# A cross-attention kernel: the value products are issued after the pair of value projections of their quarter, next to the score wave that follows

## The chip, the cores and the metric

The kernel runs on one core of one Trainium2 chip. The time is the device time of one execution in microseconds (us). Before the change it was 1936.94 us, the median of three runs (1934.74 to 1937.29). The profile was taken of a further execution, which took 1937.88 us, of which 1936.1 us lie between its first and its last instruction (the span). The engines are named as in the profile: PE multiplies matrices, PEld loads PE's weights, DVE and POOL work on vectors, ACT does activations and copies and issues some DMAs, SP issues the other DMAs.

## The reference

Three layers are computed for 16 batches of 64 query rows of width 1024: cross attention to a context of 1024 rows per batch, self-attention with rotary positions, and a quantized feed-forward layer. The change lies in the first one.

```python
def _L0_xattn_ref(query, key, value, Wq, Wk, Wv, Wo):   # key = value = the context
    q = (query @ Wq).reshape(b, sq, 32, 32).transpose(0, 2, 1, 3)
    k = (key @ Wk).reshape(b, sk, 8, 32).transpose(0, 2, 1, 3)
    v = (value @ Wv).reshape(b, sk, 8, 32).transpose(0, 2, 1, 3)
    k = jnp.repeat(k, 4, axis=1)
    v = jnp.repeat(v, 4, axis=1)
    scores = jnp.einsum('bhqd,bhkd->bhqk', q, k) * 32 ** (-0.5)
    probs = jax.nn.softmax(scores, axis=-1)
    out = jnp.einsum('bhqk,bhkd->bhqd', probs, v)
    return out.transpose(0, 2, 1, 3).reshape(b, sq, 1024) @ Wo

x = x + _L0_xattn_ref(_layernorm(x), ctx, ctx, Wq, Wk, Wv, Wo)
x = x + attn(_layernorm(x))
x = x + ffn(_layernorm(x))
```

## The kernel before

The program is recorded in the order in which the code issues it (`manual_schedule`, line 905): each engine executes its own instructions in that order, and semaphores are set wherever one needs what another makes. So the order of the Python calls is the order of the work on each engine.

**Units and slots.** Cross attention is cut into 32 units, one for each batch and each half of the heads (`class Unit`, line 416). The loop at line 939 runs 32 slots. In slot n the unit n is finished while the scores of unit n+1 (`following`) are made; slot n therefore holds work of two units. The profile's span from 187 us to 1340 us is this loop up to its last slot. A slot has four quarters, i = 0 to 3 (line 963). In each quarter these come in turn on PE:

- a *wave* of scores for the following unit (`by_key`, line 421; matmuls of line 430): eight products of 32 rows by 128 columns of weights with 256 columns of queries. Four of them use four row groups of the array side by side. The scores lie in two PSUM tiles of one buffer each, from which ACT copies them (line 442) while DVE keeps a running maximum over keys (lines 446 and 449). The next wave can only be written when both have read this one.
- two *fillers* (`fill`, line 900), taken from a list. In slots 0 to 29 the list holds the projections of the next batch's context: in quarters 0 and 1 the two halves of one 128x512 key projection each (line 225), in quarters 2 and 3 two *value steps* each, `v_0` to `v_3` (`values` within `project`, line 308; eight 128x128 products with 256 columns, line 311, then a copy by ACT, line 318). They share two PSUM banks (`ps_m`), taken in turn. In slots 30 and 31 the fillers are halves of the output projection of the first tiles (`project_out`, line 523) and a layer norm.
- between the two fillers, in quarters 2 and 3, the *value products* of unit n (`Unit.values`, line 484; matmuls of line 491): 16 products of a 128x32 weight with 256 columns of probabilities, four side by side in four column groups. Quarter 2 has the waves 0 and 1, quarter 3 the waves 2 and 3. In quarter 0 of the next slot, behind its two fillers, `finish` (line 499) adds the sums of probabilities (line 501) and divides (line 508).

One matmul of the code is recorded twice (the operands are 32-bit), so 8 products of a value step are 16 records, a wave has 16 and the value products of a quarter 32.

**The softmax and its detour through memory.** `exponentials` (line 472) subtracts the maxima on DVE (line 475), takes the exponential on ACT (line 476) and adds on POOL (lines 479 and 482). The maxima must be the same for all partitions. At the end of quarter 3, `reduce` (line 451) brings them together on DVE, its last instruction being line 461. Then ACT's queue writes 4 KB of them to device memory (`spread`, line 467) and reads them back into all partitions (`everywhere`, line 470). Below this write and this read are called the *bounce*. ACT's copies of the next wave stand behind both in ACT's order, so they wait until the write has landed.

**Loads.** The context comes in halves of 2 MB (`load_context`, line 290; the DMA is issued on SP's queue, line 207) into two buffers that are used in turn. At the start of an even slot the half for the next odd slot is issued; it overwrites the half that the four value steps of the odd slot just ended have read, and SP waits for the last of those matmuls. SP also carries the weight pieces of the feed-forward layer that are treated along the way (`load_piece`, line 365: 688 KB at line 369; from slot 8 on they are also written back, line 386).

The p buffers (`p_ring`, line 190: seven places, four per unit) are written by ACT's copies of line 442; the copies of wave 3 take the place of wave 0 of the unit that is being finished, which the value products of quarter 2 read.

Of the kernel before, what the change touches and what calls it, by code (L numbers as in the profile page):

```python
# [49 lines left out]
def kernel(  # L50
# [151 lines left out]
    def load_x(dst, t):  # L202
        nc.sync.dma_start(dst, x[bass.ts(t, P), :])

    def load(src):
        st = stream.next([KC, 512])
        nc.sync.dma_start(st, src)
        return st
# [81 lines left out]
    def load_context(b, h):  # L290
        ctx_halves[b, h] = load(ctxT[b, h])

    def project(b):


        kT = kv_ring.next([2, NK])
        v = kv_ring.next([8, KVD])
        key_steps, value_steps = [], []

        def keys(h, g):  # L300
            return matmul_steps(
                lambda: m_tile(f"k_{b}_{h}_{g}"),
                lambda k: wkvs[:, k, bass.ts(g, P)],
                lambda k: ctx_halves[b, h][:, k, :],
                lambda ps: nc.scalar.copy(kT[:, g, bass.ts(h, 512)], ps),
            )

        def values(h, kt):
            ps = m_tile(f"v_{b}_{h}_{kt}")
            for k in range(KC):  # L310
                nc.tensor.matmul(  # L311
                    ps[:, :KVD],
                    lhsT=ctx_halves[b, h][:, k, bass.ts(kt, P)],
                    rhs=wkvs[:, k, KVD:],
                    start=(k == 0),
                    stop=(k == KC - 1),
                )
            nc.scalar.copy(v[:, h * 4 + kt, :], ps[:, :KVD])  # L318

        for h in range(2):  # L320
            key_steps.append(keys(h, 0) + keys(h, 1))
            value_steps.append([lambda h=h, kt=kt: values(h, kt) for kt in range(4)])
        return kT, v, key_steps, value_steps
# [48 lines left out]
    def treat_piece():  # L372
        if not loaded:
            return
        i, m, c, st = loaded.pop(0)
        if i < len(pieces_of_w):
            nc.scalar.activation(st, st, AF.Abs, accum_out=asum[:, m, c : c + 1])
        else:


            nc.scalar.activation(
                st, st, AF.Identity, scale=inverse[:, m : m + 1], bias=magic[:, 0:1]
            )
            q = place(ternary_at, [HALF], F8)
            nc.scalar.activation(q, st, AF.Sign, bias=magic[:, 1:2], saturate=False)
            nc.sync.dma_start(half_of(ternary[m][c // 2], c), q)
        if i + 2 not in (len(pieces_of_w), len(pieces_of_w) + 1):
            load_piece(i + 2)
# [134 lines left out]
    def project_out(t, h):  # L523
        cols = bass.ts(h, 512)
        return matmul_steps(
            lambda: m_tile(f"wo_{t}_{h}"),
            lambda k: outputs[k // 4][:, t, k % 4, :, :],
            lambda k: wos[h][:, k, :],
            lambda ps: nc.vector.tensor_tensor(xs[t][:, cols], ps, xs[t][:, cols], ALU.add),
        )  # L530
# [20 lines left out]
    def norm2(t):  # L551
        n2s[t] = n2_ring.next([DIM])
        for step in layernorm(n2s[t], xs[t], f"n2_{t}"):
            step()
# [345 lines left out]
    def fill(n=1):  # L900
        for _ in range(n):
            if fillers:
                fillers.pop(0)()

    with tc.manual_schedule():
# [14 lines left out]
        unit, last = Unit(0, kT, v), None  # L920
# [18 lines left out]
        for n in range(2 * B):  # L939

            b = n // 2
            if n % 2 == 0:
                fill(len(fillers))
                if b + 1 < B:
                    load_context(b + 1, 1)
                    kT, v, key_steps, value_steps = project(b + 1)
                    tiles.append((kT, v))
                    for h in range(2):
                        fillers += key_steps[h] + value_steps[h]
                else:  # L950
                    for t in range(4):
                        load_x(xs[t], t)
                    nc.sync.dma_start(wkvs2, wkv2)
                    for h in range(2):
                        for t in (4, 5):
                            fillers += project_out(t, h)
                    for t in (0, 1):
                        for h in range(2):
                            fillers += project_out(t, h)
                        fillers += [lambda t=t: norm2(t)]  # L960
            following = Unit(n + 1, *tiles[(n + 1) // 2]) if n + 1 < 2 * B else None

            for i in range(4):
                if following:
                    following.by_key(i)
                    if i == 3:
                        following.reduce()
                if n < 8 or i % 2 == 0 and (n, i) != (8, 0) or i == 3 and n % 2 == 1:
                    treat_piece()
                if n == 8 and i < 2:  # L970
                    (thresholds, thresholds_end)[i]()
                if i == 1 and n % 2 == 1:

                    if b + 2 < B:
                        load_context(b + 2, 0)
                    elif b + 2 == B:
                        wos.append(load(wo[0]))
                fill()
                if i == 1:
                    unit.exponentials(0)  # L980
                if i == 2:
                    unit.exponentials(2)
                    unit.values((0, 1))
                if i == 3:
                    unit.values((2, 3))
                if following and i == 3:
                    following.spread()
                fill()
                if following and i == 3:
                    following.everywhere()  # L990
                if last and i == 0:
                    last.finish()
                if i == 1:
                    unit.exponentials(1)
                if i == 2:
                    unit.exponentials(3)
            if n == 2 * B - 4:
                for t in (4, 5):
                    load_x(xs[t], t)
            if n == 2 * B - 3:  # L1000
                wos.append(load(wo[1]))
            if n == 2 * B - 2:
                for t in (6, 7):
                    load_x(xs[t], t)
            last, unit = unit, following
# [194 lines left out]
```

## Time and profile before

| | us |
|---|---|
| median of three runs | 1936.94 |
| profiled execution | 1937.88 |
| its span | 1936.1 |
| PE busy in the span | 1906.5 (98%) |
| DVE busy | 1162.8 (60%) |
| ACT busy | 893.5 (46%) |
| POOL busy | 835.9 (43%) |
| key projections on PE (line 225, k) | 472.2 |
| value projections (line 311) | 460.5 |
| score waves (line 430) | 146.7 |
| value products (line 491) | 125.5 |
| sum products (line 501) | 20.4 |

The busy times are unions of overlapping instructions: a matmul record of 379 ns does not mean that the next one starts 379 ns later. What one more matmul costs is read from the distance between starts. The granted clock of PE was 0.997 of full speed on the mean. "idle before" counts the idle time of an engine just before a group and names what ended it; an idle time of DVE, ACT or POOL matters only where PE then waits for them.

### The profile page before, as it was taken

The page shows a single profiled execution, that of the slowest core. Times are in us where ns is not written, and L with a number is a line of the kernel's source. Part 1 is how long each engine was busy: PE and PEld are TensorE (multiplying, and loading weights), DVE is VectorE, ACT ScalarE, POOL GpSimd, SP SyncE. Part 2 cuts the span into 40 slices and gives each one's busy share as a digit, 9 for nine tenths or more (in the row PEclk, how much of TensorE's full clock was granted, in tenths as well). Part 3 has the DMA queues.
Part 4 walks back from the last instruction along what each step waited for, and adds up shares of the span by engine and source line. Part 5 has one row for each costly group of instructions (what it writes and reads, how often), then busy time and mean ns, then how long its engine had stood idle before and what let it go on. Part 6 is the DMA issues. An engine that isn't in the chain of part 4 may idle for free.

```text
span 1936.1 us, 27466 instructions
## 1 busy us (share of the span) xinstructions
PE 1906.5 (98%) x11632; PEld 1112.1 (57%) x11632; DVE 1162.8 (60%) x1336; ACT 893.5 (46%) x972; POOL 835.9 (43%) x411
## 2 busy tenths in 40 slices
PE   8999999999999999999999999999899999999999
PEld 5445566566556656656665565564346464666654
DVE  3012777777677767767767676777424245665564
ACT  1243665666566666666656666543101022333221
POOL 1000466456446546645654565466302423444420
PEclk9999999999999999999999999999999999999999
DMA  8224344353343342343343333314011000122201
GB/s 333 73 88 170 103 169 141 126 174 110 118 166 110 120 172 97 123 164 110 128 146 125 113 110 129 119 55 166 8 48 44 0 30 1 31 74 89 85 23 55
DMA packets 47946, 205.52 MB, mean 106 GB/s; under 512 B 7056, under 2 KB 16208, under 8 KB 42832
## 3 DMA queue, kind: packets, MB, share of 16 engines
q1 hardware_dynamic: 40528, 184.77, 27.4%
q10 hardware_dynamic: 7296, 19.01, 2.9%
q8 instruction: 91, 1.49, 0.3%
q14 instruction: 31, 0.25, 0.0%
HBM read 190.98 MB, written 12.78 MB: 105 GB/s over the span
## 4 chain that ended last, share of the span: by engine, by line
PE 83%; DVE 9%; ACT 3%; DMA 3%; issue 1%; POOL 0%; ACTq 0%; DVEq 0%; POOLq 0%
PE k L225 19%; PE v L311 18%; PE q L225 11%; PE t L430 6%; PE wo L225 5%; PE o L491 5%; PE gu L809 4%; PE d L883 4%; DVE arena L475 4%; PE g L809 3%; DMA tops<-arena 2%; DVE arena L449 2%; ACT arena L476 1%; PE v L589 1%; ACT arena L442 1%
## 5 line engine op out<-in xcount | busy, mean ns | idle before, releaser
L482 POOL TENSOR_TENSOR arena<-arena 128x1024 f32<-128x1024 f32 x192 | 574.3, 2991 | 24.9 <-ACT arena L476 9.9
L225 PE MATMUL k<-arena 128*128 128x512 f32 x1056 | 472.2, 600 | 0.0
L311 PE MATMUL v<-arena 128*128 128x256 f32 x1984 | 460.5, 385 | 0.0
L311 PEld LDWEIGHTS v<-arena 128*128 128x128 f32 x1984 | 367.0, 190 | 90.1 <-issue 45.1
L475 DVE TENSOR_TENSOR arena<-arena 128x2048 f32<-128x2048 f32 x128 | 364.0, 2882 | 0.0
L479 POOL TENSOR_TENSOR arena<-arena 128x1024 f32<-128x1024 f32 x32 | 77.6, 2426 | 650.9 <-ACT arena L476 449.7
L449 DVE TENSOR_TENSOR arena<-t,arena 128x512 f32<-128x512 f32 x384 | 262.3, 689 | 151.7 <-ACT arena L442 99.7
L225 PEld LDWEIGHTS k<-arena 128*128 128x128 f32 x1056 | 195.9, 190 | 242.1 <-issue 236.0
L476 ACT ACTIVATE arena<-arena 128x2048 f32<-128x2048 f32 x128 | 244.8, 1912 | 177.2 <-DVE arena L475 177.2
L442 ACT COPY arena<-t 128x1024 f32<-128x1024 f32 x256 | 248.7, 1012 | 167.0 <-DMA tops<-arena 89.6
L225 PE MATMUL q<-arena 128*128 128x512 f32 x512 | 225.4, 596 | 0.6 <-ACT arena L262 0.6
L446 DVE TENSOR_REDUCE arena<-t 128x512 f32<-128x1024 f32 x64 | 78.0, 1224 | 215.3 <-PE t L430 120.2
L225 PEld LDWEIGHTS q<-arena 128*128 128x128 f32 x512 | 95.3, 190 | 115.9 <-issue 113.7
L430 PE MATMUL t<-arena 32*128 32x256 f32 x2048 | 146.7, 400 | 4.1 <-DVE arena L446 4.1
L430 PEld LDWEIGHTS t<-arena 32*128 32x128 f32 x2048 | 92.5, 184 | 68.2 <-issue 47.6
L491 PE MATMUL o<-arena 128*32 128x256 f32 x2048 | 125.5, 384 | 6.1 <-ACT arena L476 6.1
L809 PEld LDWEIGHTS <-arena 128*128 128x128 bf16 x1024 | 97.6, 97 | 55.0 <-issue 5.0
L821 POOL TENSOR_TENSOR arena<-arena 128x344 f32<-128x344 f32 x64 | 70.8, 1108 | 104.8 <-DVE arena L818 95.5
L225 PE MATMUL wo<-arena 128*128 128x512 f32 x256 | 114.9, 604 | 0.0
L318 ACT COPY arena<-v 128x256 f32<-128x256 f32 x124 | 45.8, 369 | 117.9 <-DVE arena L461 90.4
L491 PEld LDWEIGHTS o<-arena 128*32 128x32 f32 x2048 | 59.8, 110 | 63.6 <-issue 17.6
L508 DVE RECIPROCAL arena<-o 128x256 f32<-128x256 f32 x32 | 56.2, 1755 | 64.9 <-PE o L501 64.7
(129 smaller groups left out, 1559.4 us busy)
## 6 DMA issues: line engine op xcount, KB each, us to landing
arena<-in_ctxT SPq DMA_DIRECT2D x31, 2048.0 KB, 9.0
arena<-in_wg SPq DMA_DIRECT2D x32, 688.0 KB, 4.2
arena<-in_wu SPq DMA_DIRECT2D x32, 688.0 KB, 4.2
arena<-in_wd SPq DMA_DIRECT2D x32, 688.0 KB, 4.2
arena<-tops ACTq DMA_DIRECT2D x32, 512.0 KB, 4.0
arena<-ternary SPq DMA_DIRECT2D x32, 344.0 KB, 3.6
ternary<-arena SPq DMA_DIRECT2D x48, 172.0 KB, 1.9
arena<-in_x SPq DMA_DIRECT2D x16, 512.0 KB, 9.9
```

The lines of the kernel that those rows point to most:

```text
L225: nc.tensor.matmul(made[0], lhsT=lhsT(k), rhs=rhs(k), start=(k == 0), stop=(k == KC - 1))
L311: nc.tensor.matmul(ps[:, :KVD], lhsT=ctx_halves[b, h][:, k, bass.ts(kt, P)], rhs=wkvs[:, k, KVD:], start=(k == 0), stop=(k == KC - 1),)
L430: nc.tensor.matmul(ws[jj // 2][:, jj % 2, a, :], lhsT=self.kT[rows, self.g, bass.ts(i * 2 + a, P)], rhs=qa[self.g][rows, bass.ts(self.b, 2 ...
L442: nc.scalar.copy(pt[:, 2 * mine : 2 * mine + 2], ws[mine])
L446: nc.vector.tensor_reduce(m, w.rearrange("p j a c -> p j c a"), AX.X, ALU.max)
L449: nc.vector.tensor_tensor(m, w[:, :, a], m, ALU.max)
L475: nc.vector.tensor_tensor(pt, pt, by.to_broadcast([P, 4, 2, 256]), ALU.subtract)
L476: nc.scalar.activation(pt, pt, AF.Exp)
L479: nc.gpsimd.tensor_tensor(acc, pt[:, :, 0], pt[:, :, 1], ALU.add)
L482: nc.gpsimd.tensor_tensor(acc, acc, pt[:, :, a], ALU.add)
L491: nc.tensor.matmul(self.po[bass.ts(jj, HD), 0:256], lhsT=self.v[:, kt, bass.ts(self.g * 4 + jj, HD)], rhs=self.pts[i][:, jj, a, :], start= ...
L809: nc.tensor.matmul(ps[:, :CW], lhsT=xqT[t][:, k, :], rhs=wbs[n][i][:, k, :], start=(k == 0), stop=(k == KC - 1),)
```

## The change

The value products of quarters 2 and 3 move from their place between the two fillers of the quarter to a place behind the second filler, so that they stand directly before the next wave (or before the next slot's first wave). The two value steps of the quarter then follow one another. Within quarter 2 they also come behind `exponentials(3)`, whose instructions run on DVE, ACT and POOL. The number of instructions on every engine is the same, and the orders of DVE, ACT, POOL and SP are as before; only PE's order differs.

```diff
@@ -980,9 +980,6 @@
                     unit.exponentials(0)
                 if i == 2:
                     unit.exponentials(2)
-                    unit.values((0, 1))
-                if i == 3:
-                    unit.values((2, 3))
                 if following and i == 3:
                     following.spread()
                 fill()
@@ -994,6 +991,9 @@
                     unit.exponentials(1)
                 if i == 2:
                     unit.exponentials(3)
+                    unit.values((0, 1))
+                if i == 3:
+                    unit.values((2, 3))
             if n == 2 * B - 4:
                 for t in (4, 5):
                     load_x(xs[t], t)
```

PE's order in quarter 2 of slots 0 to 29, before and after (`t` a wave, `v` a value step, `o` value products):

```
before: t_2  v_0  o(0,1)  v_1  t_3
after:  t_2  v_0  v_1  o(0,1)  t_3
```

In slot 31, which has no following unit, the order of the last fillers (`wo` half steps) and value products changes in the same way:

```
before: o(0,1)  wo wo  o(2,3)  wo wo ...
after:  wo  o(0,1)  wo wo  o(2,3)  wo ...
```

## The prediction

> **What bounds the kernel now.** First the windows of two neighbouring slots (columns: stretch, its length, busy time of PE, PEld, DVE, ACT, POOL, granted clock, DMA share, GB/s):
>
> ```profile
> 599.41:636.21 36.80, 36.80 (x232) 22.37 (x230) 27.14 (x27) 25.85 (x24) 20.60 (x9) 1.00 0.38 128
> 636.21:673.90 37.69, 37.40 (x236) 22.66 (x232) 27.45 (x27) 22.57 (x22) 20.45 (x9) 1.00 0.37 132
> ```
>
> PE has no gap in the first and 0.29 us in the second; DVE works 27 us of 37. So PE's order is what counts, and I read PE's timeline (start, length, line, records):
>
> ```profile
> 173.00 13.98 PE L311 MATMUL v<-arena 128*128 128x256 f32 x64
> ...
> 614.65 1.15 PE L430 MATMUL t<-arena 32*128 32x256 f32 x16
> 615.73 3.72 PE L311 MATMUL v<-arena 128*128 128x256 f32 x16
> 619.38 1.93 PE L491 MATMUL o<-arena 128*32 128x256 f32 x32
> 621.25 3.72 PE L311 MATMUL v<-arena 128*128 128x256 f32 x16
> 624.90 1.15 PE L430 MATMUL t<-arena 32*128 32x256 f32 x16
> ...
> 643.28 0.64 PE L501 MATMUL o<-arena,ones 128*32 128x256 f32 x8
> 644.20 1.15 PE L430 MATMUL t<-arena 32*128 32x256 f32 x16 [0.29 <-DVE arena L446]
> ```
>
> A lone value step takes 3.65 us to the start of what follows (619.38 - 615.73); four without a break take 13.90 (to the wave at 186.90), 3.48 each. The last line shows the one place where PE waits regularly: wave 1 of an even slot, for DVE's reading of wave 0. The chain of waits says why:
>
> ```profile
> 606.01 0.61 PE o L501 x8
> 606.65 1.77 DVE arena L508
> ...
> 634.88 0.37 DVE arena L461
> 635.27 6.16 DMA tops<-arena
> 641.46 0.33 ACTq L470
> 641.88 1.02 ACT arena L442
> 642.92 1.24 DVE arena L446
> 644.20 1.15 PE t L430 x16
> ```
>
> From the sum products of the odd slot to wave 1 of the even slot runs a path of DVE, the bounce and ACT that is as long as PE's own work. 6.16 us of it is a 4 KB write. The queues show what it meets (SP, then ACT):
>
> ```profile
> 634.21 0.42 SPq L369 DMA_DIRECT2D arena<-in_wg  x1
> 635.24 0.33 SPq L207 DMA_DIRECT2D arena<-in_ctxT  x1
> 680.84 0.39 SPq L207 DMA_DIRECT2D arena<-in_ctxT  x1
> ...
> 673.31 0.33 ACTq L467 DMA_DIRECT2D tops<-arena  x1
> 674.67 0.33 ACTq L470 DMA_DIRECT2D arena<-tops  x1
> ```
>
> At the end of the even slot nothing is loaded and the write is over in 1.36 us (673.31 to 674.67). At the end of the odd slot (635.27) a weight piece and a 2 MB context half were issued 1.06 and 0.03 us before it.
>
> **The change, part by part.** *PE's switches.* By the starts of single records, matmuls of a value step follow one another in 216 ns; the first takes 320 and the last 309 until the next shape starts. Waves and value products enter and leave in the same way. The order t v o v t has four switches, t v v o t three: one exit (309 - 216 = 93 ns) and one entry (320 - 216 = 104 ns) fall away, 0.197 us a quarter. That presumes that o to t, which the trace does not have, costs what it did after v. Nearest rows: line 501, the same 128x32 shape, to a wave takes 309 ns where PE does not wait, and that wave is again 1.08 us long. Bounds: nothing saved, or a further 197 ns if o to t needed no switch; I take the row. Two quarters make 0.394 us a slot: PE's share of a slot falls from 37.33 (644.20 to the next wave 1 at 681.53) to 36.94.
>
> *Odd slots.* Wave 1 of slots 1 to 27 is reached with 2.4 to 5.1 us to spare after DVE's line 446. All of the saving counts: 14 x 0.394 = 5.5 us.
>
> *Even slots.* Here the path competes. Measured from wave 1 to wave 1 it takes, in slots 2, 4, 6, 8: 37.28, 37.10, 37.39, 36.80; 10 to 26: 37.84, 37.68, 37.64, 36.83, 37.58, 37.68, 37.96, 39.54, 37.06; 28 and 30: 36.12, 36.30; slot 29, where an output weight is loaded instead, 37.41. A slot takes the larger of this and PE's need. If the path stays, the gain is the sum of max(37.33, path) - max(36.94, path), 2.1 us, not 16 x 0.394.
>
> *But the path moves.* The context half is released by the last matmul of v_3. That used to end with the quarter; now o(2,3) follows, 1.86 us, and the whole slot is 0.39 shorter, so it is free some 2.3 us before the bounce. In slots 10 to 26 SP itself arrives at line 207 only 0.54 us before the bounce, behind the weight piece; in 2 to 8, 28, 29 and 30 the full 2.3 us count. What an earlier load does to the 4 KB write I read from the DMA packets, engine by engine. Issued 0.03 to 0.05 us ahead, one context packet of 16 KB (611 ns) stands before the write's first packet, behind 6 to 8 packets of the weight piece; issued 0.10 to 0.11 ahead (slots 2 to 8), three do. Lead costs queue. Each of the write's two packets and its completion then lets one more context packet past. How long can the queue get? The 512 KB read-backs at the starts of slots 8, 28 and 30 were issued into long queues: on the mean of the engines 67, 66 and 69 KB in 11 to 13 packets stood before their first one, which came 2.9 us later than in a free queue. Today's write in slots 10 to 26 has 48 to 57 KB in 7 to 8 packets before it and comes 2.4 to 2.8 us late. If a queue is full at some 67 KB, there is room for about 13 KB, 0.5 us at 16 KB in 611 ns. If it is full at a count, there is room for up to four context packets, 2.4 us. Below nothing the shift can go as well, since a load begun earlier also ends earlier: with 2.3 us of lead perhaps to -1 us. I take 0.5 in slots 10 to 26, because the delay, too, is already within half a us of the full queues', and 0.3 in the others. Then the even slots lose 3.6 us instead of gaining 2.1.
>
> [...] Here packets of the two queues alternate singly once both are there.
>
> *Slots 30 and 31.* In slot 30 one switch goes (0.2) and so does the wait of o(2,3) for its exponential (0.29): 0.5 us. In slot 31 PE stands still for an exponential:
>
> ```profile
> 1371.31 1.93 PE L491 MATMUL o<-arena 128*32 128x256 f32 x16 [5.00 <-ACT arena L476]
> ```
>
> A half output step (8 records, 8 x 0.43 = 3.4 us) now comes before this wait instead of after the last one. The exponentials there hang on DVE and POOL, not on PE's order, so the step is free: 3.4 us, bounded by nothing and 5.0.
>
> *Added waits.* v_1 now starts 1.87 us earlier and needs its bank from the key copy (line 305); in slots 10 to 30 this ends 1.08 to 1.5 us before that (0.89 in slot 9). Behind v_1 would wait all of PE, one for one. o(0,1) comes later, which only eases its wait for exponentials; ACT's copies of wave 3, which reuse what o(0,1) reads, need wave 3 anyway, which PE starts after it. DVE, ACT and POOL keep their orders.
>
> **Sum.** 5.5 - 3.6 + 0.5 + 3.4 = 5.8 us off the profiled execution's 1937.9, 1932.1. That execution stood 0.9 above the median: 1931.
>
> **Rivals.** *The bounce is pushed out (slower).* One mechanism: the context half, freed by v_3 before o(2,3), takes the queue in front of the write. At 2.0 us in slots 10 to 26 (0.7 to 0.9 elsewhere) the even slots lose 19.5 us; against 9.4 gained that is +10.1. PE then idles 2.6 to 3.0 us in six of these nine; one idle time of 2.14 us (slot 24) was followed by 3.41 us at half clock in which the key matmuls lost 1.78 us, one of 2.03 us (at 1638.65) was not, so I add half of the six: +5.3. 1952, with 1943 to 1964 for shifts of 1.5 to 2.4 and no or all clocks lost. It decides from a shift of about 1.0 us. For it: lead visibly costs queue, 0.54 us is ten times the present lead, and single engines of the read-backs had up to 17 packets in front. Against: present writes already come nearly as late as the read-backs in full queues. [...]
>
> *The bounce does not move or gets shorter (faster).* 5.5 + 2.1 + 0.5 + 3.4 = 11.5: 1925; for it, that the half's packets cannot start earlier behind the weight piece. A shift of -0.5 would make it 1920.
>
> *A wash.* A shift of 0.7 to 1.3 gives 1933 to 1941.
>
> *The change does not do what it says*, because o to t costs a switch more than the row of line 501 says. Then PE saves nothing, only 3.9 us of slots 30 and 31 are left, and the earlier release still costs: inside the wash or above it.
>
> **How the numbers follow.** Forecast 0.46 (own range 1927 to 1934), pushed-out bounce 0.34, unmoved 0.10, wash 0.10. Time 1931. 0.2%, 3.9 us, is about what a measurement of this kernel can tell from no change. Faster: 0.41 of the forecast and the unmoved 0.10, 0.51; same: 0.05 and 0.10, 0.15; slower 0.34. The range, 1925 to 1955, leaves out half of the unmoved case and the last third of the pushed-out one.
>
> **What would show it.** PE's timeline: v x32 in 7.10 us and a quarter of 10.04. SP's line 207 should be issued 0.5 us before line 467 at odd slots' ends in slots 10 to 26, and no more right after PE's wave. The write's landing there tells the rivals apart: 6.1 us now, 6.6 by forecast, 8.1 by the rival. PE's idle time before line 430, 4.1 us in all now, should be near 14; near 29 and with more half clock the rival holds. At 1371 a wait of 1.5 us. Wrong would be PE waits before line 311 or a quarter still of 10.24.

## The result, and the profile after

Fourteen runs of the changed kernel have a median of 1935.24 us (1928.31 to 1940.67), fourteen of the kernel before 1937.00 (1934.74 to 1941.34). The ratio is 0.9987 with a 95% interval of 0.9975 to 0.9999: some 2.5 us less, between 0.2 and 4.8. That is less than the 0.2% (3.9 us) which the prediction took as the least that can be told from no change; the forecast was 1931, with the range from 1925 to 1955. The profiled execution took 1936.34, its span is 1934.5.

The profile's rows of the waves and the value products before the change (busy time, mean ns of one, idle time before them and what ended it):

```profile
L430 PE MATMUL t<-arena 32*128 32x256 f32 x2048 | 146.7, 400 | 4.1 <-DVE arena L446 4.1
...
L491 PE MATMUL o<-arena 128*32 128x256 f32 x2048 | 125.5, 384 | 6.1 <-ACT arena L476 6.1
```

The summary of the engines and three of the costliest groups after the change:

```profile
PE 1894.6 (98%) x11632; PEld 1117.2 (58%) x11632; DVE 1162.1 (60%) x1336; ACT 891.2 (46%) x972; POOL 835.1 (43%) x411
...
L311 PE MATMUL v<-arena 128*128 128x256 f32 x1984 | 444.4, 382 | 0.0
...
L430 PE MATMUL t<-arena 32*128 32x256 f32 x2048 | 146.6, 400 | 15.7 <-DVE arena L446 15.6
...
L491 PE MATMUL o<-arena 128*32 128x256 f32 x2048 | 124.8, 384 | 5.0 <-ACT arena L476 5.0
```

PE has 11.9 us less to do (1906.5 before): 60 quarters with 0.197 us saved in each make 11.8. But the span fell by 1.6 only, so PE stands still 10.3 us longer, and the line of the waves shows where: 4.1 us of waits before, 15.7 after, 15.6 of them for DVE's line 446. Two windows in the two slots that the prediction started from (the columns as there; neither these windows nor the prediction's have their borders at waves):

```profile
598.50:635.44 36.94, 36.94 (x233) 22.84 (x232) 27.53 (x28) 25.75 (x24) 20.80 (x8) 1.00 0.39 136
635.44:673.90 38.46, 37.20 (x234) 22.89 (x233) 27.59 (x28) 22.69 (x22) 20.45 (x7) 1.00 0.34 122
```

PE is never idle in the first and for 1.26 us in the second. From wave 1 to wave 1, the odd slot (11) fell from 37.33 to 36.94 us, as worked out; the even one (12) grew from 37.69 to 38.26. PE's timeline shows both the shorter quarter and the wait:

```profile
614.09 7.17 PE L311 MATMUL v<-arena 128*128 128x256 f32 x32
621.20 1.93 PE L491 MATMUL o<-arena 128*32 128x256 f32 x32
623.06 1.15 PE L430 MATMUL t<-arena 32*128 32x256 f32 x16
...
643.14 1.15 PE L430 MATMUL t<-arena 32*128 32x256 f32 x16 [1.25 <-DVE arena L446]
```

From the value steps to the wave after the value products (614.09 to 623.06) it is 8.97 us, and the wave before takes 1.07: a quarter of 10.04. And the chain of waits at the end of that odd slot, with SP's queue for the same stretch:

```profile
633.26 0.38 DVE arena L461
...
633.66 6.71 DMA tops<-arena
...
641.86 1.24 DVE arena L446
```

```profile
632.59 0.42 SPq L369 DMA_DIRECT2D arena<-in_wg  x1
633.11 0.39 SPq L207 DMA_DIRECT2D arena<-in_ctxT  x1
```

The context half is issued 0.55 us ahead of the write (633.11 to 633.66; before, 0.03), and the write of 4 KB lands after 6.71 instead of 6.16.

Cut at fixed points of PE's timeline, the two profiled executions differ as follows (wave 1 of unit 2 is in slot 1, wave 1 of unit 31 in slot 30, the first transposition of the second layer is the first record of line 260 behind slot 31):

| stretch, us | before | after | of it at half clock, before and after |
|---|---|---|---|
| start to wave 1 of unit 2 | 232.37 | 231.39 | |
| to wave 1 of unit 31 (the loop) | 1089.33 | 1089.52 | 3.4 and 3.4 |
| to the first transposition (slots 30 and 31) | 84.74 | 82.26 | 6.8 and 3.4 |
| to PE's end (the tail) | 525.87 | 527.59 | 0 and 3.4 |

Of the first line's 0.98 us, 0.39 are slot 1's saving. The rest, 0.59, lies ahead of the loop, where both kernels run the same instructions; this stretch differs by up to 1.7 us among the ten profiles of this document. The loop gains nothing. What the change brings comes from slots 30 and 31, and 1.7 us of it are lost again in a tail that runs the same instructions, to a stretch at half clock.

### The profile page after: what moved, and what is told of

It is laid out like the page before. It is cut to its first block, busy times and chain, and to the rows that moved or that the text cites. A ratio compares the mean times of both kernels' runs of the same rounds, so it can differ in the third digit from the quotient of the medians.

```text
span 1934.5 us, 27466 instructions
## 1 busy us (share of the span) xinstructions
PE 1894.6 (98%) x11632; PEld 1117.2 (58%) x11632; DVE 1162.1 (60%) x1336; ACT 891.2 (46%) x972; POOL 835.1 (43%) x411
## 4 chain that ended last, share of the span: by engine, by line
PE 72%; DVE 16%; ACT 5%; DMA 5%; issue 2%; POOL 0%; ACTq 0%; DVEq 0%; POOLq 0%
PE k L225 16%; PE v L311 13%; PE q L225 11%; DVE arena L475 6%; PE wo L225 5%; PE t L430 5%; DMA tops<-arena 4%; DVE arena L449 4%; PE d L883 4%; PE gu L809 4%; PE o L491 4%; PE g L809 3%; ACT arena L476 2%; ACT arena L442 2%; PE v L589 1%
## 5 line engine op out<-in xcount | busy, mean ns | idle before, releaser
L311 PE MATMUL v<-arena 128*128 128x256 f32 x1984 | 444.4, 382 | 0.0
L311 PEld LDWEIGHTS v<-arena 128*128 128x128 f32 x1984 | 372.0, 190 | 68.5 <-issue 20.4
L430 PE MATMUL t<-arena 32*128 32x256 f32 x2048 | 146.6, 400 | 15.7 <-DVE arena L446 15.6
```

Source lines behind the costliest of these rows:

```text
L311: nc.tensor.matmul(ps[:, :KVD], lhsT=ctx_halves[b, h][:, k, bass.ts(kt, P)], rhs=wkvs[:, k, KVD:], start=(k == 0), stop=(k == KC - 1),)
L430: nc.tensor.matmul(ws[jj // 2][:, jj % 2, a, :], lhsT=self.kT[rows, self.g, bass.ts(i * 2 + a, P)], rhs=qa[self.g][rows, bass.ts(self.b, 2 ...
```

## Experiments

Eight kernels were run, each timed in five rounds beside the kernel before. "Loop" is the second stretch of the table above.

| run | median (lowest to highest) | ratio to before, 95% | loop |
|---|---|---|---|
| after, half later (e1) | 1919.83 (1917.91 to 1921.48) | 0.9908, 0.9894 to 0.9921 | 1074.45 |
| before, half later (e2) | 1931.90 (1931.00 to 1932.61) | 0.9970, 0.9958 to 0.9982 | 1082.89 |
| quarter 2 alone (e3) | 1947.74 (1944.97 to 1951.11) | 1.0057, 1.0043 to 1.0070 | 1097.09 |
| quarter 3 alone (e4) | 1941.66 (1933.87 to 1946.82) | 1.0018, 1.0004 to 1.0031 | 1093.66 |
| half behind the read (e5) | 1920.52 (1919.96 to 1923.67) | 0.9911, 0.9898 to 0.9925 | 1073.75 |
| slot 31 alone (e6) | 1933.94 (1930.64 to 1939.16) | 0.9986, 0.9976 to 0.9995 | 1087.81 |
| slots 0 to 30 alone (e7) | 1936.41 (1931.99 to 1939.38) | 0.9994, 0.9985 to 1.0003 | 1088.14 |
| all loads behind the read (e8) | 1917.93 (1916.28 to 1920.91) | 0.9897, 0.9881 to 0.9914 | 1071.19 |

**The load in front of the write (e1, e2).** The theory: what the change saves on PE in the loop is lost to the context half, which now passes ahead of the write. The rival: the path over DVE and ACT would bound the even slots anyway. Both orders of PE were run with the half issued later:

```diff
                 if b + 1 < B:
-                    load_context(b + 1, 1)
                     kT, v, key_steps, value_steps = project(b + 1)
...
                     (thresholds, thresholds_end)[i]()
+                if i == 1 and n % 2 == 0 and b + 1 < B:
+                    load_context(b + 1, 1)
```

> The changed kernel, but the context half of the even slot is issued in that slot's quarter 1 instead of at its start, some 9 us after the bounce. Theory A (the gain of the switches is eaten by the write of the bounce, which queues behind the context half that v_3 now frees earlier): the write lands in 1.3 to 3 us at the ends of odd slots instead of 6 to 8, wave 1 of even slots never waits, every slot takes 36.94 us, loop from wave 1 of unit 2 to wave 1 of unit 31 29 x 36.94 = 1071 us against 1089.3 before and 1089.5 after; total near 1917. Theory B (the path of DVE and ACT bounds the even slots whatever the queue holds): the even slots stay at 37.5 to 38.5, total within 3 us of 1935.

> The kernel before, with the context half of the even slot issued in quarter 1. Theory A: the 6.8 us that the loop before spends over 29 x 37.33 go, total near 1930, and no more, since PE's order bounds it then. Theory B: same time as before, 1937.

The first took 1919.83, the second 1931.9. In the first the write lands after 1.4 to 2.7 us in slots 2 to 6 (taking the slot that follows it) and after 2.1 to 4.9 in slots 10 to 26, where the weight piece still stands ahead of it, and wave 1 does not wait there. It waits in four slots only (8, 28, 29 and 30, which take 0.66, 1.34, 0.99 and 0.26 us more than 36.94), at whose beginnings nothing holds SP back and a 2 MB load still goes out 2.1 to 2.4 us ahead of the write. In the second no wave waits, and the loop, 1082.89, is 29 x 37.33 = 1082.6 and 0.3 in slot 9: PE's order alone. So the path never bounds by itself; the write behind the load does. With that gone, the change is worth 8.4 us in the loop by the two runs, and 11.7 against the last run below, of 29 x 0.394 = 11.4 counted.

**One quarter at a time (e3, e4).** In the first only the value products of quarter 2 move, in the second only those of quarter 3 (both diffs against the kernel before). The forecast's mechanism needs quarter 3: there o(2,3) comes behind v_3 and v_3 ends earlier.

```diff
                     unit.exponentials(2)
-                    unit.values((0, 1))
                 if i == 3:
                     unit.values((2, 3))
...
                     unit.exponentials(3)
+                    unit.values((0, 1))
```

```diff
                     unit.values((0, 1))
-                if i == 3:
-                    unit.values((2, 3))
                 if following and i == 3:
...
                     unit.exponentials(3)
+                if i == 3:
+                    unit.values((2, 3))
```

> Only the value products of quarter 2 are moved, those of quarter 3 stay between the value steps, so that v_3 still ends the slot and the context half is released as before. Theory A: 0.197 us a slot from PE, the write lands as before (5 to 6.5 us); odd slots -2.8, even slots about -1.2, slot 31 -3.4: total near 1930. Theory B, in which only the number of switches counts: the loop is the same as with quarter 3 alone.

> Only the value products of quarter 3 are moved: the same 0.197 us a slot from PE, but the context half is released before them as in the changed kernel. Theory A: the write lands in 6 to 8 us, wave 1 of even slots waits as in the changed kernel; odd slots -2.8, even slots +5.5 to +6, slot 31 near 0: total near 1940, slower than quarter 2 alone by some 7 us in the loop up to slot 30. Theory B: the loop is the same as with quarter 2 alone.

The second's time came out as expected, 1941.66: half of the saving, all of the loss. The first missed by 18 us: 1947.74, the slowest of all, so that the expected order of the two is reversed. Two things went against it in its profiled run (1944.97). Slots 30 and 31 take 85.55 us, 0.8 more than before, instead of gaining 3.4: PE's wait before wave 1's products in slot 31 falls to 1.56, but a new one of 5.83 stands before wave 2's. And the loop takes 7.8 us more than before instead of 4 less. SP's queue and ACT's for the end of slot 5 of that run:

```profile
410.20 0.33 SPq L207 DMA_DIRECT2D arena<-in_ctxT  x1
```

```profile
410.52 0.33 ACTq L467 DMA_DIRECT2D tops<-arena  x1
418.18 0.33 ACTq L470 DMA_DIRECT2D arena<-tops  x1
```

And the same places of the changed kernel:

```profile
407.62 0.33 SPq L207 DMA_DIRECT2D arena<-in_ctxT  x1
```

```profile
409.99 0.33 ACTq L467 DMA_DIRECT2D tops<-arena  x1
416.59 0.33 ACTq L470 DMA_DIRECT2D arena<-tops  x1
```

With quarter 2 alone the half goes out 0.32 us (410.20 to 410.52) ahead of the write (0.10 before, 2.37 after the change), and the write takes 7.58 us, a microsecond more than after the change. The lead is not fixed by o(2,3) alone: the write hangs on DVE's path, v_3 on PE, and the 0.2 us that PE saves here bring v_3 forward by as much against the write. What the lead does, by the time from the write's issue to its first packet, is this (slots counted by the one that follows):

| lead of the half, us | slots 2 to 8: first packet, landing | lead | slots 10 to 26, behind a weight piece: first packet, landing |
|---|---|---|---|
| none ahead (e8) | 0.82 to 0.83; 1.34 to 3.05 | none ahead (e8, seven slots) | 2.0 to 2.3; 3.3 to 4.4 |
| 0.10 (before) | 2.7 to 2.8; 5.2 to 5.7 | 0.03 to 0.05 (before) | 2.8 to 3.3; 5.3 to 8.0 |
| 0.31 (e3) | 3.7 to 4.4; 6.1 to 7.6 | 0.22 to 0.26 (e3) | 3.3 to 4.0; 5.9 to 7.8 |
| 2.37 (after) | 3.4 to 3.5; 5.9 to 6.7 | 0.55 (after, six slots) | 3.5 to 3.9; 6.2 to 8.2 |

In slots 2 to 8 the delay rises steeply within the first third of a microsecond of lead and is smaller again at 2.4. So the shorter lead was worse there: 4.9 of the 7.8 us that the loop loses with quarter 2 alone are lost in these four slots. Behind a weight piece the two leads (0.22 to 0.26 and 0.55) delay the write about alike, but after the change only in six of the nine slots. Why a longer lead costs less in slots 2 to 8 is open.

**Parts of the change (e6, e7).** Slot 31 alone, and slots 0 to 30 alone:

```diff
                     unit.exponentials(2)
+                if i == 2 and following:
                     unit.values((0, 1))
-                if i == 3:
+                if i == 3 and following:
                     unit.values((2, 3))
...
                     unit.exponentials(3)
+                if i == 2 and not following:
+                    unit.values((0, 1))
+                if i == 3 and not following:
+                    unit.values((2, 3))
```

That is the edit for slot 31; the other has `following` and `not following` exchanged.

> The kernel before, with the value products behind the second filler in slot 31 alone, where no unit follows. Theory A (the half output step fills PE's wait for an exponential, as forecast): PE's wait of 5.0 us before the value products of waves 2 and 3 falls to 1.6, the loop is as before; 3.3 us less, 1933.6, a ratio of 0.9983. Theory B (the wait is given back later in the tail, or by a stretch at half clock after the new waits): the two norms and transposes that follow end at the same time; 1936 to 1938.

> The changed order in slots 0 to 30, the old one in slot 31. Theory A (odd slots gain 5.5 us, even slots lose 4 to 5.6 because the write is late in slots 2 to 8 and 28 to 30 as well): the loop ends 0 to 1.5 us earlier than before, 1935.5 to 1937. The forecast on record (even slots lose 3.6, slot 30 gains 0.5) would make it 1934.5. Theory B (the pushed-out bounce as first priced, even slots lose 19): 1947. Slot 31's own 3.3 us are missing from all three.

Slot 31 alone brings 2.7 us by the ratio (1.0 to 4.6), the rest 1.2 (from a gain of 2.9 to a loss of 0.6); the two together, 3.9, fit the whole change's 2.5. The second's 1936.41 is within theory A's range. The loops of these two profiles have no half clock, and give the cleanest comparison of the two orders: 1087.81 for the old, 1088.14 for the new, one execution each. The loop's gain is nil. In slot 31 PE's timeline goes on as follows behind the wait of 5.00 us that the prediction shows, before:

```profile
1373.17 8.98 PE L225 MATMUL wo<-arena 128*128 128x512 f32 x16
1382.08 1.07 PE L491 MATMUL o<-arena 128*32 128x256 f32 x16
1383.97 1.07 PE L491 MATMUL o<-arena 128*32 128x256 f32 x16 [0.82 <-ACT arena L476]
```

And after, from the same wait on:

```profile
1369.82 1.07 PE L491 MATMUL o<-arena 128*32 128x256 f32 x16 [1.56 <-ACT arena L476]
1370.82 7.13 PE L225 MATMUL wo<-arena 128*128 128x512 f32 x16
1380.35 1.07 PE L491 MATMUL o<-arena 128*32 128x256 f32 x16 [2.39 <-ACT arena L476]
1382.49 1.71 PE L491 MATMUL o<-arena 128*32 128x256 f32 x16 [1.07 <-ACT arena L476]
```

The wait of 5.00 falls to 1.56, but the next products now wait 2.39 for the next exponential: up to wave 3's products the exponentials set the pace (62.3 us from wave 1 of unit 31 before, 61.6 after). What is gained comes behind them, where one half step fewer is left: 22.5 us to the first transposition before, 20.7 after and 19.5 with slot 31 alone. Theory A's time was right. Its account of the wait was not: the wait of 5.00 stands before wave 1's products, not before those of waves 2 and 3, and the 1.6 that it falls to is not all that is left.

**A version that beats both (e5, e8).** If only the order of load and write counts, the half, and the two output weights (`wo`) of the last slots, can be issued on ACT's queue right behind the read. The new lines are shown; the old places of these loads, and slot 0, whose half goes to quarter 1, are left out:

```diff
                 if following and i == 3:
                     following.everywhere()
+                    if n % 2 == 1 and b + 2 < B:
+                        load_context(b + 2, 1, nc.scalar)
+                    if n == 2 * B - 4:
+                        wos.append(load(wo[0], nc.scalar))
+                    if n == 2 * B - 3:
+                        wos.append(load(wo[1], nc.scalar))
```

> The changed order of PE, and every context half that is loaded at an odd slot's end (and both output weights) issued on ACT's queue behind the read of the bounce (line 470), so that no 2 MB load is ahead of the 4 KB write. Theory A (the early release of the half is all that the change loses in the loop): the write lands after 1.4 us in slots 2 to 8 and 28 to 30, after 3.3 to 4.9 in slots 10 to 26 behind the weight piece; wave 1 never waits; 29 slots of 36.94 make 1071.2 us from wave 1 of unit 2 to wave 1 of unit 31 (1074.4 with the half in quarter 1 of the slot, where slots 8, 28, 29 and 30 still had early loads and 2.8 us of waits). Time 1917. Theory B (where the half is issued matters less than that 2 MB pass near the bounce): the half's packets or the 0.3 us of one more issue on ACT delay ACT's copies, wave 1 waits again in many even slots, and the time is 1920 or more.

All slots up to 29 take 36.94, which is theory A; but the time missed by 3.5 us. At the end of slot 29 another 2 MB load (second-layer weights) goes out 0.43 us ahead of the write, which lands after 6.36; PE waits 2.49 us at wave 1 of slot 30, and 6.8 us at half clock follow. The last run moves that load too:

```diff
-                    nc.sync.dma_start(wkvs2, wkv2)
...
+                    if n == 2 * B - 2:
+                        nc.scalar.dma_start(wkvs2, wkv2)
```

> As the run with the halves behind the read of the bounce, and the last early load too (2 MB of the second layer's weights, issued 0.43 us ahead of the write at the end of slot 29) goes behind a read, that of slot 30. Theory A (only loads ahead of the write make PE wait, and the half clock follows a long wait): the write of slot 29's end lands after 1.4 to 2.8 instead of 6.36; the wait of 2.49 at wave 1 of slot 30 and the 6.8 us at half clock that followed it there (wave 1 to wave 2 took 11.22 instead of 8.14) are gone: 2.5 + 3.1 = 5.6 less than the 1920.5 of that run, 1915, every slot 36.94. Theory B (the slot's wait comes from something else, or the later load makes the tail wait): 1918 or more.

Its group of waves reads:

```profile
L430 PE MATMUL t<-arena 32*128 32x256 f32 x2048 | 146.7, 400 | 0.0
```

No wave waits; the loop is 1071.19, 29 x 36.94 to 0.1 us, 18.1 less than before. The time is 1917.93, 1.0% less than before (0.9 to 1.2%), 2.9 above the expectation. That expectation took 5.6 off the other run's median, while the wait that it was worked out from stood in its profiled run, which took 1923.67; the two profiled runs differ by 5.4. Whether this version or the first one of this section is the faster their intervals do not tell.

## Why the prediction was right or wrong

*PE's switches: right.* Value products to a wave took 309 ns, the row of line 501; v x32 7.11 us from start to start, a quarter 10.04, a slot 36.94.

*Odd slots, 5.5 us: right.* In the changed kernel every odd slot up to 27 takes 36.94 but slot 19, which runs in part at half clock (38.63), as slot 25 did before (39.02). PE's busy time fell by 11.9 us, with 11.8 counted.

*The lead: right.* Line 207 is issued 0.55 us ahead of the write in slots 10 to 26, but for slot 22, and 2.37 in slots 2 to 8.

*Even slots, 3.6 us: here the forecast failed, by 2 us.* The mechanism was the right one (a load that passes ahead of the write makes PE wait, as the moved loads show), the shift was mis-sized. By the intervals from wave 1 to wave 1 the even slots and slot 29 lost 5.6. In slots 10 to 26 they lost 2.2 where 3.7 was counted: six writes landed 0.8 us later on the mean (the estimate was 0.5; the one in slot 24 landed 0.4 earlier), but in three slots the write came early: in 22 the issue of the weight piece held SP for 1.95 us instead of 0.42, and the half went out 0.98 us behind the write; in 10 and 16 the write's first packets came at 2.1 and 2.3, and why is open. The run with slots 0 to 30 alone has early writes in the same three slots. The forecast had no reason for them, and in that its number was lucky: with 0.8 in all nine slots they would have lost 6.4 by the forecast's own sum, an estimate, and the kernel would have been some 4 us slower. In slots 2 to 8 they lost 2.5 where 0.4 was counted, and in 28 to 30 they lost 0.9 where 0.5 was to be gained. The term that failed is "0.3 in the others": the write moved by 0.8 us in slots 2 to 8 (5.19 to 5.71 became 5.93 to 6.71) and by 1.2 in 28 to 30. The rows that could have sized it stood in the trace of before: the first packets of the three read-backs in the longest queues came at 3.4 to 3.6 instead of 0.97, about 2.5 late (the prediction's 2.9 is a mean over the DMA engines). So the first packet of a write behind as long a queue comes at about 0.83 + 2.5 = 3.3, an estimate. In slots 2 to 8 it came at 2.7 before, which leaves room for 0.6, not 0.3; it came at 3.4 to 3.5. That this is no upper bound the run with quarter 2 alone shows, at 3.7 to 4.4; a length at which a queue is full, from which the prediction took its 0.5, no run shows. That a load begun earlier also ends earlier, which made the estimate smaller, no row of before had shown. In the changed kernel the half does so: begun 2.37 us ahead of the write in slots 2 to 8, its last packet ends 5.0 to 6.8 us behind the write's issue instead of 7.6 to 8.3. The write lands later all the same.

*The rivals.* The pushed-out bounce has the right mechanism, at 0.8 to 1.2 us instead of 2.0. That packets of the two queues alternate is seen after the change too: from the write's first packet to its second it is 0.62 to 0.74 us in slots 2 to 8 of both traces (medians of 16 pairs), about one 16 KB packet of the half, which takes 0.61. "A wash", a shift of 0.7 to 1.3 and 1933 to 1941, is what came, at a chance of 0.10; the forecast's own range, 1927 to 1934, was missed. That the change does not do what it says is refuted by the quarter of 10.04.

*Slots 30 and 31, 3.9 us: the half step right, the rest of the sum off by 1.4 in the profile.* They brought 2.5, with slot 31 alone 3.0. The exponentials, which were taken not to move, do not; but the prediction left 1.5 us of the old wait and counted no new one, and 2.39 us of new wait stand before wave 2's products. The 3.41 us at half clock that follow there fit the 1.2 by which the end of slot 31 is longer than with slot 31 alone (20.7 and 19.5).

*The tail.* 1.7 us of the gap between the profiled 1936.3 and the 1932.1 worked out are a stretch at half clock at 1628.5, which the forecast counted for the rival alone.

Together: 2.0 in even slots, 1.4 in slots 30 and 31 and 1.7 in the tail make 5.1 against a gap of 4.2; the 0.6 ahead of the loop and slot 9, which took 37.58 before instead of the 37.33 counted, make up the rest.

## What to carry to other kernels

Work saved on the bounding engine can bring forward a load that it releases (here 2 MB, issued up to 2.4 us ahead of a 4 KB write instead of 0.11 at most), while a path on other engines goes on as before; before counting the saving, list what the engine's last instruction of the stage sets free and what that meets in the DMA queues. A small transfer on a critical path is best kept ahead of the large ones by the order of issue: here it took 15 to 17 us off the changed kernel, which had gained 2.5 by PE's order. When a row of the trace shows how late a transfer comes in a long queue (here 2.5 us), take that delay as the size to expect, not a fraction of the way to it; with quarter 2 alone it came up to 1.1 us later still.

## What was not expected of the hardware

*The half clock kept to a grid in these ten profiles.* In each of them all stretches that the trace shows at half clock begin a whole number of 3.413 us apart (the first two of before 273.07 us, 80 times that; of after 512.00, 150 times). Windows of before and after on that grid (columns as above; the clock stands behind the five engines), each pair the window of a wait and the next one. Before:

```profile
1093.62:1097.03 3.41, 1.27 (x21) 0.73 (x17) 2.36 (x2) 3.37 (x4) 0.00 (x0) 1.00 0.45 166
1097.03:1100.44 3.41, 3.41 (x8) 1.50 (x5) 2.81 (x5) 3.41 (x4) 0.00 (x0) 0.50 0.35 82
```

After:

```profile
1092.64:1096.05 3.41, 1.58 (x11) 0.34 (x9) 0.98 (x1) 2.03 (x3) 0.00 (x0) 1.00 0.62 222
1096.05:1099.47 3.42, 3.12 (x21) 1.78 (x22) 3.35 (x5) 3.39 (x4) 0.00 (x0) 1.00 0.07 25
```

PE waited 2.14 us in the first case and 2.13 in the second. The first wait lay within one window (PE busy for 1.27 us of it), the second was cut by a border (busy 1.58, and 3.12 in the next), and only the first was followed by half clock. Behind the first 10 us of the program every window of the ten profiles with 1.895 us or more without PE was followed by half clock, and of fourteen with 1.70 to 1.89 us only one (nearest to the border: 1.90 at 872.73 with quarter 2 alone, followed, and 1.89 at 1632.56 with slot 31 alone, not followed). That fits the two waits that the prediction could not put in order: the one of 2.03 us at 1638.65 was cut into 1.11 and 0.92 by a border. Where the grid falls differs from run to run (its first border lies 1.35 us behind the span's start before, 0.38 after), and so does the time at half clock, which a kernel's times follow: the changed kernel's fastest runs (1928.3 and 1928.5 us) had a mean clock of 1.000, its slowest (1938.4 to 1940.7) one of 0.996. Not explained: in the tail five of the ten profiles drop to half clock after a window with only 1.2 to 1.4 us idle (after the change 1.18 at 1625.12), and others with as much do not (1.34 at 1626.10 before).

*What one such window costs.* The tail runs the same instructions in all ten profiles. It takes 525.87 to 525.89 us in the four without half clock, 527.53 to 527.59 in the five with one window, 530.91 in the one with three: 1.7 us a window.
